# A mixture-of-experts layer whose leftover half groups are joined to pairs, as groups of three

## The chip, the cores and the metric

The kernel runs on one core of one Trainium2 chip. The time is the device time of one execution in microseconds, and the kernel before is given as the median of four runs. A core has five engines with queues of their own: TensorE (PE; its weight loads are listed as PEld), VectorE (DVE), ScalarE (ACT), GpSimd (POOL) and SyncE (SP), which here issues transfers only. POOL issues the transfers whose rows are chosen by a list.

## What is computed

A gated transformer layer on 8 x 512 tokens of width 256, everything in float32: cross-attention with 16 heads, then a router that sends each token to two of eight experts, each a two-layer network of inner width 1024.

```python
x = x + jnp.tanh(g_xattn[0]) * _L0_xattn_ref(_layernorm(x), ctx_1024, ctx_1024, mask, ...)
x = x + jnp.tanh(g_ffn[0]) * _L0_ffn_ref(_layernorm(x), router_w, router_b, expert_up, expert_down)

def _L0_ffn_ref(x, router_w, router_b, expert_up, expert_down):
    x_flat = x.reshape(-1, D)
    probs = jax.nn.softmax(x_flat @ router_w + router_b, axis=-1)
    top_w, top_idx = jax.lax.top_k(probs, TOP_K)
    comb = jnp.sum(top_w[..., None] * jax.nn.one_hot(top_idx, E, dtype=x.dtype), axis=1)
    output = jnp.zeros_like(x_flat)
    for e in range(E):
        h = jax.nn.gelu(x_flat @ expert_up[e].T, approximate=False)
        output = output + comb[:, e:e + 1] * (h @ expert_down[e].T)
    return output.reshape(B, S, D)
```

## The kernel before

**Attention, then experts, in one stream.** `attend_near` walks over the batches. While batch b's attention runs, the finished batch's rows are normalised and routed. Each routed token gets two entries in a table in memory, one for each expert it goes to; an entry says which row it is and with what weight it counts. The table has a region per expert, filled from its start (`filled` counts the rows of each expert so far). 64 indirect transfers on POOL (line 378) write it. It is first cleared by one transfer (`clear_table`, line 148), so that an empty slot points at no row.

**Groups.** The experts don't run over all tokens, but over groups of table rows of one expert. A half is 128 rows. A pair is two halves, 256 rows; a single is one half. Which groups exist is known only at run time, so `plan(k)` works it out with short VectorE operations for four kinds k: 5 pairs after three batches, 12 more pairs after six, 15 pairs after all eight, and then singles, of which the odd half of an expert makes one. Four singles always run (`OFTEN`), four more stand in a conditional block at the end (`compute_extra`, line 789), which is entered when more than four experts have an odd half. The plans give each group an expert (`whose_i`) and a place in the table (`line_i`).

**Jobs.** `JOBS` (lines 54 to 60) is the fixed order of the groups: 17 pairs, then 15 pairs with a single after the third, sixth, ninth and twelfth of them; 36 jobs in the main stream. The first four are mixed by hand into the attention of batches 4 to 7 (`amid`, line 1015). The others run after it (line 1087), the first of them interleaved with what is left of the last batches' routing (`queue`).

**One job.** `list_rows` (line 685) reads the group's table rows into `listed`; `load` (697) fetches the expert's two weight matrices, 1 MB each, both on SP's queue, into one of three buffers; `fetch` (713) gathers the token rows into `xg`, one POOL transfer per half; `turn` (719) transposes them on TensorE (line 724) and copies them to `xT` on DVE (726). `go_up` (729) does the first layer: 16 products, each two TensorE instructions (line 736), whose moving operand is as wide as the group has rows; ACT's Gelu (740) writes `hT`. `fetch_y` (742) gathers the rows of `out` that this group will add to. `go_down` (748) does the second layer for one half: 8 products of 128 x 128 weights against 256 columns, two TensorE instructions each (line 754), then DVE adds the weighted result to `y` (757) and POOL scatters `y` to `out` (760).

**Order.** `compute(s)` (line 771) sets the program order of a turn: gather rows of job s+2, gather `y` of job s-1, up of job s, transposes of job s+1, the downs of job s-1, list of job s+3, weights of job s+2. The framework places every instruction on its engine's queue by a schedule made from this order, and each queue is then worked in that order. All gathers of `y` read `out`, and all scatters write it, so a job's gathers wait for the scatters of the job before to land, and its scatters wait for its gathers. The scatters of the first and second halves go to views that are declared disjoint (`out_parts`, line 79).

**Banks.** The accumulators of a half's down (`o_ps`) come from `bank`, two buffers; those of up (`h_ps`) from five; the transposes' `x_ps` from one.

Of the kernel before, what the change touches and what calls it, by code (L numbers as in the profile page):

```python
# [10 lines left out]
F32 = mybir.dt.float32  # L11
# [8 lines left out]
P = 128  # L20
# [14 lines left out]

TOKENS = B * S
GROUP = 2 * P
PAIRS = 2 * TOKENS // GROUP
SINGLES = E

TABLE = TOKENS // GROUP


PARTS = (3, 6, B, B)
ENDS = [-(-(b * S * 2 - E * (GROUP - 1)) // GROUP) for b in PARTS[:2]] + [PAIRS]
SIZES = [ENDS[0], ENDS[1] - ENDS[0], ENDS[2] - ENDS[1], SINGLES]

OFTEN = SINGLES // 2

TABLES = E * TABLE + SIZES[2]  # L50

# [3 lines left out]
for _n in range(SIZES[2]):  # L55
    JOBS.append((2, _n))
    if _n % 3 == 2 and _n // 3 < OFTEN:
        JOBS.append((3, _n // 3))
MAIN = len(JOBS)
JOBS += [(3, n) for n in range(OFTEN, SINGLES)]  # L60
# [3 lines left out]
def flamingo_layer(ctx: ExitStack, tc: tile.TileContext, a: dict, out: bass.AP):  # L64
# [11 lines left out]
    table = tc.dram_tile([TABLES * GROUP, ENTRY], I32, name="table")  # L76

    table_parts = dram_disjoint_views(table, B * QT * 2)
    out_parts = dram_disjoint_views(out, 2)
# [68 lines left out]
    def clear_table(t):  # L148

        many = t.rearrange("p (n c) -> p n c", c=ENTRY)[:, : TABLES * GROUP // P // 11]  # L150
        nc.gpsimd.memset(many, 0)
        nc.gpsimd.memset(many[:, :, 0], TOKENS)
        nc.gpsimd.memset(many[:, :, 1], TOKENS - 1)
        n = many.shape[1]
        nc.sync.dma_start(
            out=table.rearrange("(p r n) c -> p r (n c)", p=P, n=n),
            in_=t[:, : n * ENTRY].unsqueeze(1).to_broadcast([P, TABLES * GROUP // P // n, n * ENTRY]),
        )
# [8 lines left out]
    full_i = mk.tile([P, 2 * TABLE], I32, tag="full_i", name="full_i")  # L167
    nc.gpsimd.iota(full_i, pattern=[[P, 2 * TABLE]], base=0, channel_multiplier=0)
    full = fixed([P, 2 * TABLE], "full")
# [13 lines left out]
    nc.vector.tensor_scalar(filled, iota, float(TOKENS), None, ALU.mult)  # L183
# [406 lines left out]
    def experts(pool, seen, half_bank, bank, row_bank):  # L590
# [6 lines left out]
        tables, loaded, fetched, turned, made, ys = {}, {}, {}, {}, {}, {}  # L597

        def halves(s):
            return 1 if JOBS[s][0] == 3 else 2  # L600

        def plan(k):
            n = SIZES[k]
            single = k == 3
            w = 1 if single else 2
            lines = 2 * TABLE // w

            def planned(shape, name, dtype=F32):
                return plans.tile(shape, dtype, tag=f"{name}{k}", name=f"{name}{k}")

            def scratch(shape, name):
                return plans.tile(shape, F32, tag=name, name=f"{name}{k}")

            def count():

                count = scratch([P, E], "count")
                nc.vector.scalar_tensor_tensor(count, iota, -float(TOKENS), filled, ALU.mult, ALU.add)  # L620
                if not single:
                    nc.vector.tensor_scalar(count, count, 1.0 - GROUP if k < 2 else -float(P), None, ALU.add)
                more = scratch([P, E, lines], f"more{lines}")
                nc.vector.tensor_tensor(
                    more, count.unsqueeze(2).to_broadcast([P, E, lines]),
                    full[:, ::w].unsqueeze(1).to_broadcast([P, E, lines]), ALU.is_gt,
                )
                groups = scratch([P, E + 1], "groups")
                nc.vector.memset(groups[:, E:], 0.0)
                nc.vector.tensor_reduce(groups[:, :E], more, AX.X, ALU.add)  # L630
                if k:
                    nc.vector.scalar_tensor_tensor(groups, tables["done"], -2.0 / w, groups, ALU.mult, ALU.add)
                ahead = scratch([P, E + 1, E], "ahead")
                nc.vector.tensor_tensor(
                    ahead, lower, groups[:, :E].unsqueeze(1).to_broadcast([P, E + 1, E]), ALU.mult
                )
                begin = scratch([P, E + 1], "begin")
                nc.vector.tensor_reduce(begin, ahead, AX.X, ALU.add)

                line = scratch([P, E + 1], "line")
                nc.vector.scalar_tensor_tensor(line, iota_e, float(lines), begin, ALU.mult, ALU.subtract)
                if k:
                    nc.vector.scalar_tensor_tensor(line, tables["done"], 2.0 / w, line, ALU.mult, ALU.add)
                past = scratch([P, n, E + 1], f"past{n}")
                nc.vector.tensor_tensor(
                    past, slot[:, :n].unsqueeze(2).to_broadcast([P, n, E + 1]),
                    begin.unsqueeze(1).to_broadcast([P, n, E + 1]), ALU.is_ge,
                )  # L650
                whose = scratch([P, n], f"whose{n}")
                nc.vector.tensor_reduce(whose, past, AX.X, ALU.add)
                whose_i = planned([P, n], "whose_i", I32)
                nc.vector.tensor_scalar(whose_i, whose, -1.0, float(E - 1), ALU.add, ALU.min)
                nc.vector.tensor_tensor(past, past, line.unsqueeze(1).to_broadcast([P, n, E + 1]), ALU.mult)
                far = scratch([P, n], f"far{n}")
                nc.vector.tensor_reduce(far, past, AX.X, ALU.max)
                line_i = planned([P, n], "line_i", I32)
                nc.vector.tensor_tensor(line_i, far, slot[:, :n], ALU.add)
                tables[k] = (whose_i, line_i, planned([P, n, w, FIELDS], "listed", I32))  # L660
                if single:
                    tables["extra"] = planned([P, 1], "extra", I32)
                    nc.vector.tensor_scalar(tables["extra"], begin[:, E:], float(OFTEN), None, ALU.is_gt)
                else:
                    done = planned([P, E + 1], "done")
                    nc.vector.tensor_scalar(done, begin, -1.0, float(n), ALU.mult, ALU.add)
                    nc.vector.tensor_scalar(done, done, 0.0, None, ALU.max)
                    nc.vector.tensor_tensor(done, done, groups, ALU.min)
                    if k:
                        nc.vector.tensor_tensor(done, done, tables["done"], ALU.add)  # L670
                    tables["done"] = done

            return count
# [11 lines left out]
        def list_rows(s):  # L685
            _, line_i, listed, n = planned_for(s)
            w = halves(s)
            lines = E * 2 * TABLE // w + SIZES[JOBS[s][0]]
            line = number(line_i, n, lines - 1)
            nc.sync.dma_start(  # L690
                out=listed[:, n],
                in_=table[: lines * w * P].rearrange("(r h p) c -> p r h c", h=w, p=P)[
                    :, bass.ds(line, 1), :, :FIELDS
                ].rearrange("p o h c -> p (o h) c"),
            )
# [16 lines left out]

        def fetch(s):
            xg = gather.tile([P, 2, D], F32, tag="xg", name=f"xg{s}")
            for h in range(halves(s)):
                rows_of(rows, s, h, xg[:, h, :])
            fetched[s] = xg

        def turn(s):
            xg, w = fetched.pop(s), halves(s)  # L720
            ps = row_bank(f"x_ps{s}").rearrange("p (c r) -> p c r", c=DC)
            for dc in range(DC):
                for h in range(w):
                    nc.tensor.transpose(ps[:, dc, h * P : (h + 1) * P], xg[:, h, dc * P : (dc + 1) * P], ident)  # L724
            xT = gather.tile([P, DC, GROUP], F32, tag="xT", name=f"xT{s}", bufs=2)
            nc.vector.tensor_copy(xT[:, :, : w * P], ps[:, :, : w * P])  # L726
            turned[s] = xT

        def go_up(s, f):
            up, xT, n = loaded[s][0], turned[s], halves(s) * P  # L730
            if f == 0:
                made[s] = hpool.tile([P, FC, GROUP], F32, tag="hT", name=f"hT{s}")
            ps = half_bank(f"h_ps{s}_{f}").rearrange("p (i r) -> p i r", i=2)
            for i in range(2):
                for dc in range(DC):
                    nc.tensor.matmul(  # L736
                        ps[:, i, :n], lhsT=up[:, dc, (f + i) * P : (f + i + 1) * P], rhs=xT[:, dc, :n],
                        start=(dc == 0), stop=(dc == DC - 1),
                    )
            nc.scalar.activation(made[s][:, f : f + 2, :n], ps[:, :, :n], AF.Gelu)  # L740

        def fetch_y(s):

            ys[s] = gather.tile([P, 2, D], F32, tag="y", name=f"y{s}", bufs=2)
# [20 lines left out]
        def ups(s):  # L765
            return [lambda f=f: go_up(s, f) for f in range(0, FC, 2)]
# [4 lines left out]
        def compute(s, end, first):  # L771
# [5 lines left out]
            if s + 1 < end:  # L777
                steps.append(lambda: turn(s + 1))
            if s > first:
                steps += downs(s - 1)  # L780
# [8 lines left out]
        def compute_extra():  # L789
            some = nc.values_load(  # L790
                tables["extra"][0:1, 0:1], min_val=0, max_val=1, skip_runtime_bounds_check_because="it is a comparison"
            )
            with tc.If(some == 1):
# [626 lines left out]
```

## Time and profile before

| what | value |
|---|---|
| median of 4 runs (848.88 to 855.85) | 851.57 us |
| the profiled execution | 850.44 us |
| its span, first to last instruction | 848.7 us |
| its mean granted TensorE clock | 0.954 |
| busy: PE, PEld, DVE, ACT, POOL | 766, 568, 328, 252, 314 us |
| up matmuls (L736), 1024 of 256 columns and 128 of 128 | 244.6 us |
| down matmuls (L754), 1088 of 256 columns | 244.1 us |
| gathers of rows, gathers of `y`, scatters | 68 each |
| loads of `up` and of `down`, 1 MB each | 36 each |

The span is the time from the first instruction to the last of one profiled execution; its whole time lies a little above it. Busy times of one engine are merged, so that overlapping matmuls count once. A group of instructions is listed by its line in the kernel, its engine, and the tile it writes and reads, such as `o_ps<-down,hT`; PE's own share is high over the whole span, but what ends last in a stage has to be read in that stage.

### The profile page before, as it was taken

To read this page: it belongs to the slowest core of one execution; us is meant where nothing else is said; L and a number is where in the kernel's file an instruction comes from. 1 tells how busy PE (TensorE), PEld (TensorE's weight loads), DVE (VectorE), ACT (ScalarE), POOL (GpSimd) and SP (SyncE) were. 2 spreads that over 40 slices of the span, in tenths; PEclk is the share of its full clock that TensorE was granted. 3 is DMA by queue.
4 is the path that set the end of the run, shared out by engine and by line. 5 is a ranking of instruction groups with operands and counts; after the bars stand their busy time and mean duration, and the time that the engine had idled before them with its cause. 6 is when DMAs were issued, how large, how long until landed. Compare 5 with 4: busy or idle time off the path is not lost. (4 is left out here: it accounts for less than half of the span.)

```text
span 848.7 us, 11331 instructions
## 1 busy us (share of the span) xinstructions
PE 765.9 (90%) x4090; PEld 567.9 (67%) x4090; DVE 327.6 (39%) x958; ACT 252.4 (30%) x485; POOL 313.6 (37%) x422
## 2 busy tenths in 40 slices
PE   3867989888899999899999799999999999999992
PEld 1333444434446575667787688888898988989882
DVE  7496887858865647525230111111111111011100
ACT  2434555444645435253311111111112111111210
POOL 2030115141645252444464544434342524434332
PEclk9897998989989998999999899999999999999996
DMA  4700000101293314061746656665667676757511
GB/s 143 259 7 1 32 32 29 50 29 51 88 312 99 105 53 125 4 205 50 258 138 209 200 202 214 201 207 203 194 205 236 196 240 210 227 174 258 199 50 36
DMA packets 87909, 121.58 MB, mean 143 GB/s; under 512 B 16797, under 2 KB 71712, under 8 KB 87840
## 3 DMA queue, kind: packets, MB, share of 16 engines
q1 hardware_dynamic: 75184, 93.44, 33.3%
q0 software_dynamic: 11840, 26.76, 10.1%
q8 instruction: 36, 0.59, 0.3%
q10 hardware_dynamic: 816, 0.53, 0.2%
q14 instruction: 33, 0.27, 0.1%
HBM read 101.05 MB, written 20.17 MB: 143 GB/s over the span
## 5 line engine op out<-in xcount | busy, mean ns | idle before, releaser
L754 PE MATMUL o_ps<-down,hT 128*128 128x256 f32 x1088 | 244.1, 382 | 8.7 <-DVE y L757 7.6
L736 PE MATMUL h_ps<-xT,up 128*128 128x256 f32 (+1 forms) x1152 | 244.6, 369 | 3.5 <-DMA up<-in_upT 1.8
L754 PEld LDWEIGHTS o_ps<-down,hT 128*128 128x128 f32 x1088 | 205.1, 191 | 40.8 <-DVE y L757 8.3
L736 PEld LDWEIGHTS h_ps<-xT,up 128*128 128x128 f32 x1152 | 208.7, 191 | 35.0 <-issue 6.0
L740 ACT ACTIVATE hT<-h_ps 128x512 f32<-128x512 f32 (+1 forms) x144 | 81.8, 573 | 363.6 <-PE h_ps L736 290.4
L757 DVE SCALAR_TENSOR_TENSOR y<-o_ps,listed,y 128x256 f32<-128x256 f32 x68 | 32.7, 483 | 274.9 <-DMA y<-out,listed 120.3
L708 POOL DMA_INDIRECT y<-out,listed x68 | 66.3, 975 | 165.1 <-DMA out<-y,listed 135.1
L760 POOL DMA_INDIRECT out<-y,listed x68 | 68.8, 1012 | 97.5 <-DVE y L757 70.2
L873 DVE TENSOR_REDUCE tops<-t_ps 128x4 f32<-128x512 f32 x128 | 79.4, 681 | 19.4 <-PE t_ps L868 16.0
L903 ACT ACTIVATE n_pT<-w_ps 128x512 f32<-128x512 f32 x128 | 67.5, 598 | 61.0 <-PE w_ps L898 37.3
L708 POOL DMA_INDIRECT xg<-rows,listed x68 | 64.8, 954 | 41.3 <-issue 18.5
L378 POOL DMA_INDIRECT table<-entries,place_i x64 | 62.7, 980 | 25.9 <-issue 16.5
L726 DVE COPY xT<-x_ps 128x512 f32<-128x512 f32 (+1 forms) x36 | 23.7, 658 | 106.4 <-PE x_ps L724 92.4
L898 PE MATMUL w_ps<-ql,km 32*128 32x512 f32 x256 | 54.9, 722 | 0.5 <-DVE tops L873 0.5
L868 PE MATMUL t_ps<-k,q 32*128 32x256 f32 x512 | 42.3, 404 | 3.0 <-ACT n_pT L903 1.6
L850 POOL TENSOR_TENSOR x<-x,bo 128x1024 f32<-128x1024 f32 x8 | 18.7, 2346 | 65.2 <-issue 34.5
L937 PE MATMUL proj_ps<-woT,oT 128*128 128x256 f32 x128 | 33.9, 403 | 9.8 <-DVE oT L930 9.8
L868 PEld LDWEIGHTS t_ps<-k,q 32*128 32x128 f32 x512 | 26.0, 185 | 24.7 <-issue 15.5
L916 PE MATMUL n_av<-n_pT,nv 128*32 128x512 f32 x256 | 39.1, 687 | 2.4 <-DVE xT L726 2.3
L922 DVE STREAM_TRANSPOSE raw<-n_av 128x512 f32<-128x512 f32 x32 | 22.8, 713 | 45.4 <-PE n_av L916 32.7
L937 PEld LDWEIGHTS proj_ps<-woT,oT 128*128 128x128 f32 x128 | 23.9, 197 | 21.8 <-DVE oT L930 11.4
L570 PE MATMUL q_ps<-n_xnT,wqT 128*128 128x512 f32 x64 | 34.6, 669 | 0.0
(187 smaller groups left out, 557.3 us busy)
## 6 DMA issues: line engine op xcount, KB each, us to landing
up<-in_upT SPq DMA_DIRECT2D x36, 1024.0 KB
down<-in_downT SPq DMA_DIRECT2D x36, 1024.0 KB
out<-x SPq DMA_DIRECT2D x8, 512.0 KB
rows<-xn_f SPq DMA_DIRECT2D x8, 512.0 KB
x<-in_x SPq DMA_DIRECT2D x7, 512.0 KB
table<-none SPq DMA_DIRECT2D x1, 2288.0 KB
xg<-rows,listed POOLq DMA_INDIRECT x68
y<-out,listed POOLq DMA_INDIRECT x68
```

The costliest lines, as they stand in the source:

```text
L378: nc.gpsimd.indirect_dma_start(out=table_parts[2 * t + i][:, :], out_offset=bass.IndirectOffsetOnAxis(ap=place_i[:, t, i : i + 1], axis=0) ...
L708: nc.gpsimd.indirect_dma_start(out=dst, out_offset=None, in_=src[: seen[JOBS[s][0]], :], in_offset=bass.IndirectOffsetOnAxis(ap=listed[:, ...
L736: nc.tensor.matmul(ps[:, i, :n], lhsT=up[:, dc, (f + i) * P : (f + i + 1) * P], rhs=xT[:, dc, :n], start=(dc == 0), stop=(dc == DC - 1),)
L740: nc.scalar.activation(made[s][:, f : f + 2, :n], ps[:, :, :n], AF.Gelu)
L754: nc.tensor.matmul(ps, lhsT=hT[:, f, h * P : (h + 1) * P], rhs=down[:, f, :], start=(f == 0), stop=(f == FC - 1))
L760: nc.gpsimd.indirect_dma_start(out=out_parts[h][:, :], out_offset=bass.IndirectOffsetOnAxis(ap=listed[:, n, h, 0:1], axis=0), in_=y[:, h, ...
L868: ins = nc.tensor.matmul(ps[j][:, u], lhsT=q[rows_j, c, t * P : (t + 1) * P], rhs=k[rows_j, c], start=True, stop=True)
L873: nc.vector.tensor_reduce(top[:, 2 * tp : 2 * tp + 2, :].rearrange("p t (i x) -> p t i x", i=2)[:, :, :, 32 * j], ps[j], AX.X, ALU.max,)
L898: ins = nc.tensor.matmul(ps[j], lhsT=km[rows_j, c, i, :], rhs=lowered[b, c][rows_j, i, :], start=True, stop=True)
L903: nc.scalar.activation(pT[:, j, :], ps[j], AF.Exp)
L916: ins = nc.tensor.matmul(av[32 * j : 32 * j + 32, :], lhsT=made_of(b)[3][:, 8 * c + 2 * j + r, :], rhs=pT[:, j, :], start=True, stop=True,)
L937: nc.tensor.matmul(ps[:, t - ts[0], :], lhsT=outs[b, c][:, t * P : (t + 1) * P], rhs=w["woT"][:, c, :], start=(c == 0), stop=(c == DC - 1),)
```

## The change

The fourth kind of group, the single, is gone. An expert with an odd number of halves has one group of three halves, a triple; all other groups are pairs. There are four places for triples (`TRIPLES`), and the kinds are now: 5 pairs, 12 pairs, 4 triples, 18 pairs. Of the last 18, 11 always run; three and then four more stand in two nested conditional blocks. `JOBS` is 17 pairs, then 11 pairs with a triple after the second, fifth, eighth and eleventh: 32 jobs in the main stream.

- The table's regions are 33 halves long (`SHARE`), so that a group may start at any half; `list_rows` reads as many halves as the group has.
- `plan_rest` takes the place of the last two plans; the steps common to all pairs are in `plan_pairs`.
- A triple's tiles (`xg`, `y`, `xT`, `hT`) come from a pool of their own, `wide`, with one buffer each, in the room of the attention's working pools, which are now closed when `queue` is empty.
- Its up runs over 384 columns, one product of eight at a time to a bank instead of two; its transposes go in two steps, each with its own copy, the second after the first half's down; it has three downs.

```diff
-SIZES = [ENDS[0], ENDS[1] - ENDS[0], ENDS[2] - ENDS[1], SINGLES]
-OFTEN = SINGLES // 2
+SIZES = [ENDS[0], ENDS[1] - ENDS[0], TRIPLES, 2 * TOKENS // GROUP + E - 1 - TRIPLES - ENDS[1]]
+OFTEN = SIZES[3] - 7
+MORE = OFTEN + 3
+LINES = E * SHARE + 2 * SIZES[3]
...
-for _n in range(SIZES[2]):
-    JOBS.append((2, _n))
-    if _n % 3 == 2 and _n // 3 < OFTEN:
-        JOBS.append((3, _n // 3))
+for _n in range(OFTEN):
+    JOBS.append((3, _n))
+    if _n % 3 == 1 and _n // 3 < TRIPLES:
+        JOBS.append((2, _n // 3))
...
-    out_parts = dram_disjoint_views(out, 2)
+    out_parts = dram_disjoint_views(out, 3)
...
         def halves(s):
-            return 1 if JOBS[s][0] == 3 else 2
+            return 3 if JOBS[s][0] == 2 else 2
...
+        def plan_rest():
+            count = count_rows(2)
...
+            pairs, whole = each("pairs"), each("whole")
+            nc.vector.tensor_reduce(pairs, more[:, 0], AX.X, ALU.add)
+            nc.vector.tensor_reduce(whole, more[:, 1], AX.X, ALU.add)
+            left, odd = each("left"), each("odd")
+            nc.vector.tensor_tensor(left, pairs, tables["done"][:, :E], ALU.subtract)
+            nc.vector.tensor_tensor(odd, pairs, whole, ALU.subtract)
+            three = each("three")
+            nc.vector.scalar_tensor_tensor(three, left, 2.0, odd, ALU.is_ge, ALU.mult)
...
+            nc.vector.tensor_tensor(groups[:, :E], left, saved, ALU.subtract)
+            begin = plan_pairs(3, groups)
...
+        def turn_wide(s, dc):
+            n = halves(s) * P
+            if dc == 0:
+                turned[s] = wide[0].tile([P, DC, n], F32, tag="xT3", name=f"xT{s}")
+            ps = row_bank(f"x_ps{s}_{dc}")[:, :n]
+            for h in range(n // P):
+                nc.tensor.transpose(ps[:, h * P : (h + 1) * P], fetched[s][:, h, dc * P : (dc + 1) * P], ident)
+            nc.vector.tensor_copy(turned[s][:, dc], ps)
+
+        def go_up(s, f, m):
             up, xT, n = loaded[s][0], turned[s], halves(s) * P
             if f == 0:
-                made[s] = hpool.tile([P, FC, GROUP], F32, tag="hT", name=f"hT{s}")
-            ps = half_bank(f"h_ps{s}_{f}").rearrange("p (i r) -> p i r", i=2)
-            for i in range(2):
+                where = hpool if n == GROUP else wide[0]
+                made[s] = where.tile([P, FC, n], F32, tag=f"hT{n}", name=f"hT{s}")
+            ps = half_bank(f"h_ps{s}_{f}")[:, : m * n].rearrange("p (i r) -> p i r", i=m)
+            for i in range(m):
                 for dc in range(DC):
                     nc.tensor.matmul(
-                        ps[:, i, :n], lhsT=up[:, dc, (f + i) * P : (f + i + 1) * P], rhs=xT[:, dc, :n],
+                        ps[:, i, :], lhsT=up[:, dc, (f + i) * P : (f + i + 1) * P], rhs=xT[:, dc, :],
                         start=(dc == 0), stop=(dc == DC - 1),
                     )
...
         def ups(s):
-            return [lambda f=f: go_up(s, f) for f in range(0, FC, 2)]
+            m = 512 // (halves(s) * P)
+            return [lambda f=f: go_up(s, f, m) for f in range(0, FC, m)]
+
+        def turns(s):
+            if halves(s) == 2:
+                return [lambda: turn(s)]
+            return [lambda dc=dc: turn_wide(s, dc) for dc in range(DC)]
...
-            if s + 1 < end:
-                steps.append(lambda: turn(s + 1))
-            if s > first:
-                steps += downs(s - 1)
+            turned_next = turns(s + 1) if s + 1 < end else []
+            steps += turned_next[:1]
+            last = downs(s - 1) if s > first else []
+            steps += last[:1] + turned_next[1:] + last[1:]
...
                 if queue:
                     queue.popleft()()
+                    if not queue:
+                        heads.close()
+                        open_wide()
```

## The prediction, made before the changed kernel was run

> **What bounds the kernel now.** First the page's busy slices: each of the 40 is 21.2 us.
>
> ```profile
> PE   3867989888899999899999799999999999999992
> PEclk9897998989989998999999899999999999999996
> ```
>
> From slice 24 on (about 470 us) TensorE stands at 9 and its granted clock at 9: the expert stage is bound by TensorE. Next the chain of waits, in order of time (start, us, what): it says whether that stage's end really hangs on PE.
>
> ```profile
> 473.07 9.01 PE o_ps L754 x32
> 482.08 6.91 PE h_ps L736 x32
> 488.99 0.44 PE x_ps L724 x4
> 489.43 6.91 PE o_ps L754 x32
> ...
> 717.72 0.22 PE x_ps L724 x2
> 717.94 6.91 PE o_ps L754 x32
> 724.85 3.57 PE h_ps L736 x32
> ```
>
> It does: a pair costs 6.91 us up (L736), 6.91 down (L754) and 0.44 of transposes (L724), 14.26 in all; a single 3.57, half of 6.91 and 0.22. Then the busy table by stage (stretch; its length, then PE, PEld, DVE, ACT, POOL busy; clock; DMA share; GB/s), to find where PE still waits.
>
> ```profile
> 692.00:720.00 28.00, 27.81 (x134) 24.27 (x133) 4.04 (x8) 5.37 (x9) 9.82 (x10) 1.00 0.64 212
> 720.00:750.00 30.00, 28.64 (x153) 25.48 (x152) 3.13 (x6) 3.92 (x8) 12.74 (x13) 1.00 0.61 200
> ```
>
> From 474 us to the last matmul these are the only stretches short of full: 0.19 and 1.36 us. The timeline says what PE waited for, and shows the loop that competes with it:
>
> ```profile
> 603.28 0.98 POOL L708 DMA_INDIRECT y<-out,listed  x1 [5.37 <-issue]
> 608.35 1.02 POOL L760 DMA_INDIRECT out<-y,listed  x1 [0.30 <-issue]
> 611.20 1.00 POOL L760 DMA_INDIRECT out<-y,listed  x1 [1.83 <-DVE y L757]
> 619.60 0.98 POOL L708 DMA_INDIRECT y<-out,listed  x1 [7.40 <-DMA out<-y,listed]
> ...
> 744.47 3.72 PE L754 MATMUL o_ps<-down,hT 128*128 128x256 f32 x16 [1.36 <-DVE y L757]
> ```
>
> A job's y gathers (L708) wait until the scatters (L760) of the job before have landed, and its scatters wait for its gathers. Among pairs, last scatter to next gather took 6.3 to 8.9 us, gather to add (L757) about 3.0, and y0, y1, xg0, xg1, then the first scatter start 1.27 apart on POOL (603.28 to 608.35). That loop closes in about 13.4 us (626.00 to 638.88 is 12.88; 664.23 to 677.87 is 13.64), just under the pair's 14.26, so the first half's add runs only 0.2 to 2.2 us after its matmuls end. A single breaks this: at 638.88 the loop took 16.2 us and then 9.2 (second scatter of one pair 638.88, single's 655.03, next pair's last 664.23), 25.4 against 21.5 of PE work. From 692 to 812 us the first half's add was on average 7.0 us late (up to 11.8), and twice PE found both of its o_ps banks taken.
>
> **What the change does to this, part by part.** Routing the reference's inputs gives the experts 6, 9, 6, 10, 8, 9, 11 and 9 halves: 68, four odd, which agrees with 68 gathers of each kind and with 32 pairs and 4 singles. After: 28 pairs and 4 triples, 68 halves again. Rounded up they are 36 pairs; 17 are listed early, 8 go into triples, and 11 are left, exactly OFTEN, so no extra job runs.
>
> *Up.* Four singles and four pairs (4 x 3.57 + 4 x 6.91 = 41.92 us) become four triples. Triples by the pair's cost per column: 6.91 x 1.5 = 10.37 each, 41.46; by the line through 128 and 256 columns: 10.25, 41.0. Gain 0.46 to 0.92; I take 0.5, since 256 columns is nearer to 384.
>
> The Trainium skill (TensorE: Matmul & The Clock Gate, Back-to-back issue gap) says that the spacing of matmuls is set by weight load and stream together, about 81 ns at 128 columns and 131 at 512. By that line the three widths would cost 81, 98 and 114 ns, and four triples for four singles and four pairs, 128 instructions of each, would save an estimated 8.3 us. The trace does not agree: 112 ns at 128 columns against 216 at 256, nearly proportional.
>
> *Down and transposes.* 48 matmuls instead of 32 and 16; 12 transposes instead of 8 and 4: nothing. ACT makes eight Gelus of 384 columns per triple where the rows give 0.38 for 256 and 0.60 for 512; one falls under each four matmuls of 1.3 us. DVE's two copies of 384 columns lie between 0.42 and 0.69 each, under the downs; if that cover went, they would cost PE 1.1 per triple.
>
> *The waits that singles cause.* 0.19 + 1.36 = 1.55 us, 1.6 rounded, bounds 0 (they return elsewhere) and 1.6. I take 1.6: beside a triple PE works 6.91 + 10.37 + 0.5 = 17.8 us per turn, and the loop with a third gather (1.27) and third scatter (1.3) is about 16.
>
> *The new waits.* A triple's third down needs the bank of its own first half, free 3.46 us after the first half's matmuls end. The add there ends at lateness + 0.48, so a lateness of 0.2 to 2.2 costs nothing. The second copy of xT3 stands behind that add in the program order of DVE: 2.2 + 0.48 + 0.55 = 3.2 under 3.46 plus the transposes. On POOL a triple's three row gathers hold the scatters behind them 1.27 back, in a turn that still has 7.92 (603.28 to 611.20) for its last scatter: 7.6. Taken 0; bounds 0 and 0.6 for each of three triples.
>
> *Transfers.* Eight transfers of 1 MB fewer on SP's queue (`up` and `down` of four jobs); PE waits 1.8 us for `up` in the whole trace, so nothing on the path. Lists: one DMA per job as before.
>
> *The planning.* The last plan grows from 36 to 43 short DVE operations, 7 x 0.2 = 1.4 us, between 430 and 440 us; the jobs that read it begin some 150 us later, and the adds and copies of the stage have 7 us of down matmuls over them. The two early plans gain three operations (3 x 0.17 = 0.5) where DVE stands at 7 to 8 tenths. The cleared table grows from 286 to 300 blocks, 112 KB, 0.4 us at the 260 to 320 GB/s of that stage. I take 0.3 lost, bounds 0 and 0.9.
>
> *The end.* The last job is now a triple.
>
> ```profile
> 826.30 0.48 DVE L757 SCALAR_TENSOR_TENSOR y<-o_ps,listed,y 128x256 f32<-128x256 f32 x1 [2.97 <-PE o_ps L754]
> 830.31 0.98 POOL L708 DMA_INDIRECT y<-out,listed  x1 [2.25 <-DMA out<-y,listed]
> 833.41 0.48 DVE L757 SCALAR_TENSOR_TENSOR y<-o_ps,listed,y 128x256 f32<-128x256 f32 x1 [6.63 <-DMA y<-out,listed]
> 836.46 1.00 POOL L760 DMA_INDIRECT out<-y,listed  x1 [0.30 <-issue]
> ```
>
> Call T the end of the next-to-last job's downs (826.10). T comes 3.46 earlier, since one half more lies behind it. The add of the last job's first half starts at T + 7.3 as now; its third down can begin when that add is done, T + 7.8, takes 3.46, and its scatter follows about 1.0 later, T + 12.3 instead of T + 10.36. From the last scatter to the end 12.24 stay. Gain 3.46 - 1.95 = 1.5, bounds 0.5 and 2.
>
> Sum: -0.5 - 1.6 + 0 + 0.3 - 1.5 = -3.3 us on a span of 848.7: 845.4. The profiled execution took 850.44 in all, 1.7 more than its span and 0.13% under the median of 851.57. The same ratio on the median gives **848.3 us**. With all bounds taken at once: -4.5 to +1.7, 847.1 to 853.3.
>
> **The rivals.**
>
> *The triple ties PE to the gather loop (slower).* Now the same job's add frees the bank for its third half, where a pair has a whole turn of slack. If lateness stays at the 7.0 us of the singles' stage, each of three triples stalls 7.0 + 0.48 - 3.46 = 4.0, 12 us: 860. It beats the gain once lateness at triples passes 3.46 - 0.48 + 3.3/3 = 4.1. For it: ten of the eleven first halves from 692 us on were above 2.6. Against it: those followed singles, and the pairs before 603 us worked lateness off by about 0.9 per turn. The Trainium skill (TensorE: Matmul & The Clock Gate, Architectural detail) has VectorE's queue as strict FIFO, which speaks against this change: the copy of xT3 would wait with the add. No run here shows a copy in that place yet.
>
> *Weight loads count (much faster).* TensorE loads 1024 weights for up instead of 1152, 128 fewer; at their full 191 ns that is 24 us: 827. Against it stands 3.57 beside 6.91.
>
> *The order shifts at the last routing.* At 473 us the chain shows PE idle for 6.3 us, at 459 for 2.1, while POOL alternates between table scatters and job DMAs. The order of each engine is set by the scheduler; a longer plan can move an add there. One place in POOL's order is worth 1.3 us, three of them 4: 844 or 852, either way.
>
> *It doesn't do what it says.* With more than 11 pairs left, three extra jobs of 14.26 would run: 891. The counts exclude it.
>
> **How the numbers follow.** What a measurement of this kernel can tell from no change is 0.5%, 4.3 us. Forecast 0.66: its lower bound just passes -4.3 and the four runs shown scatter by 7 us, so 0.21 faster, 0.43 within, 0.02 slower. Loop rival 0.20: 0.14 slower, 0.06 within, when only one or two triples stall. Order rival 0.09: 0.05 faster, 0.01 within, 0.03 slower. Weight loads 0.04, faster. Extra jobs 0.01, slower. Faster 0.30, within 0.50, slower 0.20. The likeliest one's own range is 847.1 to 853.3; the one that holds 8 in 10 reaches down to 844 (order rival) and up to 857, where the loop rival costs two thirds of its price.
>
> **What would show it right or wrong.** Right: h_ps of 384 columns at 10.3 to 10.4 us per triple; no PE gap over 0.3 us from 474 us to the last `up`; the first half's add at most 2.2 us after its matmuls everywhere; at the end a gap of about 0.9 us before the third half's downs. Wrong: PE gaps of several us ahead of a triple's third half or of the `up` of a triple; a copy of xT3 behind a waiting add; a stage before 474 us that ends more than 2 us earlier or later.

## The result, and the profile after

The changed kernel takes 847.65 us (median of 38 runs) against 851.19 (59 runs): ratio 0.9955, 95% interval 0.994 to 0.997, 3.8 us faster where 3.3 were forecast. The ratio leaves out slow executions; the two medians, which don't, differ by 3.5. Two more groups of runs gave 0.998 (0.9942 to 1.0019) and 0.9962 (0.9934 to 0.9991). The profiled execution has a span of 844.9 us.

From the page of the changed kernel: the busy slices of PE with the granted clock, and the two groups of matmuls.

```profile
PE   3877989888899999999998799999999999999992
PEclk9898998888899998999999899999999999999997
...
L848 PE MATMUL o_ps<-down,hT 128*128 128x256 f32 x1088 | 245.0, 383 | 8.6 <-DVE y L851 7.5
L830 PE MATMUL h_ps<-xT,up 128*128 128x256 f32 (+1 forms) x1024 | 242.6, 393 | 3.3 <-DVE oT L1041 1.7
```

The expert stage is as full as it was. Down has the same 1088 matmuls; up has 1024 instead of 1152, but its busy time falls only from 244.6 to 242.6. From the chain of waits, in order of time (start, us, what), one triple:

```profile
601.34 0.33 PE x_ps L818 x3
601.67 3.46 PE o_ps L848 x16
605.13 0.33 PE x_ps L818 x3
605.45 3.46 PE o_ps L848 x16
608.91 10.32 PE h_ps L830 x32
619.23 0.44 PE x_ps L807 x4
619.67 6.91 PE o_ps L848 x32
...
633.92 10.36 PE o_ps L848 x48
```

Its transposes lie around the first down of the job before (601 to 605), its up takes 10.32 us, its three downs 10.36, and PE never waits. At each triple but the last, the first half's add runs as soon as its matmuls end, as here:

```profile
637.41 0.48 DVE L851 SCALAR_TENSOR_TENSOR y<-o_ps,listed,y 128x256 f32<-128x256 f32 x1 [2.77 <-PE o_ps L848]
```

The table by stage agrees (stretch; its length, then PE, PEld, DVE, ACT, POOL busy; clock; DMA share; GB/s): where the kernel before had 0.19 and 1.36 us of idle PE, every stretch from 600 to 800 us is full. One of them:

```profile
720.00:760.00 40.00, 40.00 (x176) 32.18 (x175) 4.13 (x8) 7.53 (x15) 14.11 (x15) 1.00 0.57 183
```

The end is another matter. The timeline of the changed kernel from the next-to-last job's second add (818.47) on:

```profile
818.47 0.48 DVE L851 SCALAR_TENSOR_TENSOR y<-o_ps,listed,y 128x256 f32<-128x256 f32 x1 [2.97 <-PE o_ps L848]
...
822.48 0.98 POOL L785 DMA_INDIRECT y<-out,listed  x1 [2.25 <-DMA out<-y,listed]
823.77 0.97 POOL L785 DMA_INDIRECT y<-out,listed  x1 [0.30 <-issue]
825.05 0.95 POOL L785 DMA_INDIRECT y<-out,listed  x1 [0.30 <-issue]
...
826.03 3.72 PE L848 MATMUL o_ps<-down,hT 128*128 128x256 f32 x16 [0.70 <-DVE y L851]
...
828.57 1.02 POOL L854 DMA_INDIRECT out<-y,listed  x1 [2.56 <-DMA y<-out,listed]
829.79 0.48 DVE L851 SCALAR_TENSOR_TENSOR y<-o_ps,listed,y 128x256 f32<-128x256 f32 x1 [2.75 <-PE o_ps L848]
829.89 1.01 POOL L854 DMA_INDIRECT out<-y,listed  x1 [0.30 <-issue]
831.20 0.99 POOL L854 DMA_INDIRECT out<-y,listed  x1 [0.30 <-issue]
```

The third down does wait for the bank (826.03), but the last scatter does not wait for it: POOL issues three gathers 1.28 apart, holds the first scatter until the third gather has landed, and issues three scatters 1.31 apart. Its queue ends later than the third add at 829.79.

Then POOL waits for the last scatter to land. Each line below gives POOL's waits at the very end (shortest, median and longest, in ns); the longest is the wait for that landing. The lines are from the kernel before, the changed kernel, and the kernel before with the longer gather loop of the experiments:

```profile
L793 POOLq EVENT_SEMAPHORE  x4: 17/43/2270, 836.7 to 839.2; - x4
L908 POOLq EVENT_SEMAPHORE  x5: 17/43/3471, 831.5 to 835.3; - x5
L796 POOLq EVENT_SEMAPHORE  x4: 17/43/4090, 850.6 to 854.9; - x4
```

From the start of the last scatter (836.46, 831.20 and 850.33) to the end of that wait are 2.6, 4.0 and 4.4 us. What follows the landing takes 9.6 to 9.8 us in all 14 profiles.

Three profiles of either kernel, cut at two points: "start" is where PE's 6.3 us gap after the last routing ends, T the end of the next-to-last job's downs.

| kernel, profile | start | start to T | T to end | start to end |
|---|---|---|---|---|
| before, first | 473.07 | 353.03 | 22.63 | 375.65 |
| before_2 | 466.62 | 351.77 | 22.70 | 374.47 |
| before_3 | 468.73 | 352.87 | 22.68 | 375.55 |
| changed, first | 470.49 | 347.77 | 26.68 | 374.45 |
| after_2 | 471.71 | 347.88 | 26.84 | 374.72 |
| after_3 | 470.11 | 347.45 | 27.30 | 374.76 |

Start to end agrees within 1.2 us from profile to profile of one kernel, the start itself scatters by 6.5. In the stage that the change is about, the mean falls from 375.2 to 374.6 us: 0.6, not 3.8.

### The profile page after: what moved, and what is told of

It reads as the page before. It is cut to its first block, busy times and chain, and to the rows that moved or that the text cites. A ratio compares the mean times of both kernels' runs of the same rounds, so it can differ in the third digit from the quotient of the medians.

```text
span 844.9 us, 10980 instructions
## 1 busy us (share of the span) xinstructions
PE 766.7 (91%) x3962; PEld 553.8 (66%) x3962; DVE 328.3 (39%) x968; ACT 252.4 (30%) x485; POOL 314.7 (37%) x422
## 4 chain that ended last, share of the span: by engine, by line
PE 67%; DVE 14%; issue 5%; SPq 3%; DMA 3%; ACT 2%; POOL 1%; another core or an unknown queue 0%; POOLq 0%; DVEq 0%; ACTq 0%
PE h_ps L830 24%; PE o_ps L848 24%; DVE tops L984 4%; PE w_ps L1009 4%; PE n_av L1027 3%; PE proj_ps L1048 3%; SPq L769 3%; PE t_ps L979 2%; PE q_ps L572 2%; PE top_ps L997 1%; DVE n_o L1036 1%; PE x_ps L807 1%; DVE ql L998 1%; DMA out<-y,listed 1%; DMA y<-out,listed 1%
## 5 line engine op out<-in xcount | busy, mean ns | idle before, releaser
L830 PE MATMUL h_ps<-xT,up 128*128 128x256 f32 (+1 forms) x1024 | 242.6, 393 | 3.3 <-DVE oT L1041 1.7
L830 PEld LDWEIGHTS h_ps<-xT,up 128*128 128x128 f32 x1024 | 193.2, 190 | 46.4 <-issue 5.0
L809 DVE COPY xT<-x_ps 128x512 f32<-128x512 f32 x28 | 19.3, 689 | 135.6 <-PE x_ps L807 120.1
L1009 PE MATMUL w_ps<-ql,km 32*128 32x512 f32 x256 | 58.1, 745 | 0.4 <-DVE tops L984 0.4
L572 PE MATMUL q_ps<-n_xnT,wqT 128*128 128x512 f32 x64 | 32.3, 631 | 0.2 <-ACT k L559 0.2
```

The lines of the kernel that those rows point to most:

```text
L830: nc.tensor.matmul(ps[:, i, :], lhsT=up[:, dc, (f + i) * P : (f + i + 1) * P], rhs=xT[:, dc, :], start=(dc == 0), stop=(dc == DC - 1),)
L1009: ins = nc.tensor.matmul(ps[j], lhsT=km[rows_j, c, i, :], rhs=lowered[b, c][rows_j, i, :], start=True, stop=True)
```

## The experiments

The theory: TensorE bounds the expert stage, and the change is worth what it takes from PE's columns and waits there, less what the longer last job costs at the end. The rivals: a triple ties PE to the loop of gathers and scatters; singles cost nothing beyond their matmuls; the gain comes from the planning, the table or the closed pools rather than from the groups.

**Both kernels again** (before_2, after_2, later before_3, after_3; no edit).

> The kernel before, unchanged, profiled once more. Theory: the 2.6 us by which the changed kernel reached the expert stage earlier (470.5 against 473.1 us) is scatter between executions, since the order on every engine up to there is the same but for the plans; this profile then reaches that point anywhere between 469 and 476 us, the ratio is 1.000 within its interval, and PE again waits 1 to 4 us for an o_ps bank between 680 and 770 us, in jobs that follow a single. Rival: the earlier start belongs to the change; then this profile stands at 473 again within 0.5 us.

Measured: 0.9982 (0.9938 to 1.0025). Start at 466.62, ahead of the 469 to 476 expected and 6.5 us ahead of the first profile of the same kernel, so the start scatters by more than the 2.6 us in question. PE's waits for banks came to 0.19 us, less and later than the 1 to 4 expected:

```profile
786.76 1.56 PE L754 MATMUL o_ps<-down,hT 128*128 128x256 f32 x6 [0.19 <-DVE y L757]
```

> The changed kernel, unchanged, profiled once more. Theory: 0.9955 of the time before; no PE gap over 0.3 us between the first 10 us of the expert stage and the last up; first halves added at most 1 us late at every triple; from the end of the next-to-last job's downs to the end of the span 26 us, as in the first profile. Rival (the triple ties PE to the gather loop): lateness over 3 us at some triple and a gap ahead of its third half.

Measured: 0.998 (0.9942 to 1.0019); no gap between start and the last up, the first half's add 0.2 us late at each triple of the stream, 26.84 us from T to the end.

> The kernel before, unchanged, third profile, beside the changed kernel on one chip. Theory: ratio 1.000 within its interval; 374 to 376 us from the start of the expert stage (the end of its 6.3 us gap) to the end of the span; 0 to 2 us of PE waiting for o_ps banks after singles. Rival: the time before that stage is longer here than in the changed kernel by 2 us or more.

Measured: 1.001 (0.9978 to 1.0043); 375.55 us from start to end, and one wait of 1.28 us:

```profile
689.97 1.35 PE L754 MATMUL o_ps<-down,hT 128*128 128x256 f32 x5 [1.28 <-DVE y L757]
```

> The changed kernel, unchanged, third profile. Theory: 0.994 to 0.998 of the time before; 374.4 to 374.8 us from the start of the expert stage to the end of the span, of which 26.7 after the next-to-last job's downs; the start of that stage within 3 us of that of the kernel before on the same chip, either way.

Measured: 0.9962 (0.9934 to 0.9991); 374.76 us, of which 27.30 after T. The starts of the two, 468.73 and 470.11, don't explain a faster kernel.

**The last job a pair** (after_lastpair, after_lastpair_2).

```diff
-    if _n % 3 == 1 and _n // 3 < TRIPLES:
+    if _n % 3 == 0 and _n // 3 < TRIPLES:
```

> The changed kernel with each triple one pair earlier, so that the last job is a pair. Theory: the end after the next-to-last job's downs shrinks from 26.4 to 22.4 us as in the kernel before, and one half more lies ahead of it (3.46): 0.5 us faster than the changed kernel, 0.995 of the time before. Rival (the 4 us at the end have to do with the nested conditional blocks and not with the third half): the end stays above 24 us and the kernel becomes 1 to 2 us slower than the changed one.

Measured: 0.9973 (0.9933 to 1.0014), T to end 22.72 us, start to end 373.69. So the 4 us belong to the third half of the last job, not to the nested conditional blocks, which are still there.

> The changed kernel with a pair as its last job, once more, beside the changed kernel on the same chip. Theory: 1.0 us faster than the changed kernel by the profiles (373.7 against 374.6 us from the start of the expert stage to the end), 0.993 to 0.997 of the time before. Rival: no faster than the changed kernel.

Measured: 0.9959 (0.993 to 0.9989); 372.94 us from start to end. By the profiles it beats both kernels, by 1.3 us on the changed one (373.3 against 374.6); by the times it can't be told from it (845.52 and 846.26 us beside each other).

**Singles at the end of the stream** (before_singles_end): the four singles of the kernel before run one after another.

```diff
-    if _n % 3 == 2 and _n // 3 < OFTEN:
-        JOBS.append((3, _n // 3))
+JOBS += [(3, _n) for _n in range(OFTEN)]
```

> The kernel before with its four singles moved behind all 15 pairs, nothing else: the same matmuls. Theory (a single's turn has 7.25 us of PE work, but its loop of gather, add, scatter and landing takes some 12): the lateness of the adds grows by about 5 us per single and PE stalls there 5 to 12 us in all, while the waits between 690 and 750 us vanish (-1.6) and the end after a single is about 2 us shorter net: 1.003 to 1.01. Rival (singles cost no more than their matmuls): no new gaps, and the shorter last job makes it 1 to 2 us faster, 0.998.

Measured: 1.0076 (1.0041 to 1.011): singles do cost more than their matmuls. The time is in the range of the theory, but its mechanism isn't what happened: PE waited only 0.65 us in the stream, not 5 to 12, and the rest showed at the end, 29.36 us from T on. The chain there:

```profile
829.71 5.04 DMA y<-out,listed
...
834.93 0.50 DVE y L756
...
835.69 1.00 POOL out L759
...
838.27 2.78 DMA y<-out,listed
```

Gather, landing, add, scatter, landing, and again: a single's whole loop in a row, with no matmul in it.

**Triples closer together** (after_dense): one pair between two triples, three pairs at the end.

```diff
-    if _n % 3 == 1 and _n // 3 < TRIPLES:
-        JOBS.append((2, _n // 3))
+    if _n % 2 == 1 and _n // 2 < TRIPLES:
+        JOBS.append((2, _n // 2))
```

> The changed kernel with its triples after the second, fourth, sixth and eighth of the last 11 pairs instead of the second, fifth, eighth and eleventh: one pair between two triples, and three pairs at the end. Theory (TensorE bounds the stage, and beside a triple it works 17.8 us per turn against a gather loop of 16): no new gap between first and last up, lateness under 2 us, the stage as long as with the last job a pair (373.7 us from its start to the end of the span), 0.995 to 0.998 of the time before. Rival (a triple ties PE to the gather loop): lateness builds over the dense triples, gaps of 1 us or more ahead of third halves, 2 to 6 us slower than the changed kernel.

Measured: 0.9949 (0.9926 to 0.9971), on another chip, where the kernel before takes 833.09 us. No gap, lateness at most 1.0 us, start to end 373.92. The rival fails where it should show most.

**A longer gather loop in both kernels** (before_long_loop, after_long_loop).

```diff
             for h in range(halves(s)):
                 rows_of(out, s, h, ys[s][:, h, :])
+            if s >= 17:
+                mine = ys[s][:, : halves(s), :]
+                nc.vector.tensor_scalar(mine, mine, 1.0, None, ALU.mult)
```

> The kernel before, with the gather loop lengthened in the last 19 jobs: VectorE multiplies each gathered y by one ahead of the adds, which has to wait for all its gathers. The outputs stay the same. Theory (singles cost waits because their loop does not shrink with their matmuls): a pair's loop grows by about 1.1 us to 14.5, a single's two turns from 25.4 to 27.6 against 21.5 of PE work; some 6 us of lateness per single, four of them less the 10 us that the banks cover: PE waits 10 to 18 us for o_ps banks from 650 us on, 1.012 to 1.02 of the time before. Rival (the waits that a single causes are worth nothing): under 1.003.

Measured: 1.0345 (1.0304 to 1.0387), more than expected, and not for the reason given. The timeline of before_long_loop:

```profile
629.19 0.98 POOL L708 DMA_INDIRECT y<-out,listed  x1 [7.63 <-DMA out<-y,listed]
...
636.21 0.29 DVE L749 TENSOR_SCALAR y<-y 128x256 f32<-128x256 f32 x1 [16.86 <-DMA xg<-rows,listed]
636.41 0.68 DVE L726 COPY xT<-x_ps 128x512 f32<-128x512 f32 x1
...
637.15 3.35 PE L736 MATMUL h_ps<-xT,up 128*128 128x256 f32 x7 [9.03 <-DVE xT L726]
```

The single's multiplication waits for its gather (issued at 629.19, it lands at 636.11; the row names the transfer of rows issued behind it), the next job's copy of xT waits behind it on DVE, and PE waits for the copy: 9.0 us here, 23.6 at the four singles together. It was not the o_ps banks. So it shows what a late loop costs at a single, with a wait that neither kernel has of itself.

> The changed kernel with the same multiplication by one in the last 15 jobs. Theory: pairs lose 0.3 us per turn, a triple's turns win back 0.7 or more; PE waits at most 2 us, 0 to 2 us slower than the changed kernel, and 8 to 16 us faster than the kernel before with the same lengthening. Rival (the triple ties PE to the gather loop, so that a longer loop hits it harder than the kernel before): gaps ahead of third halves, slower than the kernel before with the lengthening.

Measured: 1.0155 (1.0103 to 1.0207), 842.67 us: 18.8 faster than the kernel before with the same edit, but some 13 slower than the changed kernel, where 0 to 2 were expected. (The changed kernel has no run on that chip; its 829.3 there is an estimate, 0.9955 of 833.09.) TensorE's weight loads for the triples' second transposes wait 7.4 us in all for the one bank of x_ps, whose first copy stands behind the multiplication; the end grows by 4 to 30.8 us; and two of the three third halves in the stream wait, as here:

```profile
692.34 1.99 PE L851 MATMUL o_ps<-down,hT 128*128 128x256 f32 x8 [0.92 <-DVE y L854]
```

The first half's add was 4.0 us late there, and the rival's price says 4.0 + 0.48 - 3.46 = 1.0, where 0.92 was measured. So the rival's mechanism exists at its price; in the changed kernel, where the first half's add is 0.2 us late at each triple of the stream, its condition is never met.

**The last job a single** (before_last_single).

```diff
-    if _n % 3 == 2 and _n // 3 < OFTEN:
-        JOBS.append((3, _n // 3))
+    if _n % 3 == 2 and _n // 3 >= 1:
+        JOBS.append((3, _n // 3 - 1))
```

> The kernel before with its four singles one place later each, after the sixth, ninth, twelfth and fifteenth of the 15 pairs, so that the last job is a single. Theory (each half of the last job costs the end a gather of 1.28, a scatter of 1.31 and 1.4 of landing, all on POOL and its transfers): from the end of the next-to-last job's downs to the end of the span 18.7 us where a pair has 22.7 and a triple 26.7. Rival (what the triple's end lost is its third down waiting for the bank, 3.5 us that a single does not have either way): 21.4 us, the pair's less one gather.

Measured: 1.0022 (0.9997 to 1.0047), and 22.49 us from T to the end: both expectations miss. The timeline of POOL there:

```profile
811.70 0.98 POOL L708 DMA_INDIRECT y<-out,listed  x1 [2.51 <-DMA out<-y,listed]
816.72 1.00 POOL L760 DMA_INDIRECT out<-y,listed  x1 [4.03 <-DVE y L757]
```

The only gather (811.70) lands in 4.1 us by the chain of waits, where the last one of the kernel before takes 2.7, and 13.0 us follow the last scatter instead of 12.3. What the missing gather and scatter save, these two take back. So the end is not a fixed price per half. Why this gather lands later is open; being alone doesn't make it so, since the last single's gather in before_singles_end landed in 2.78 us.

**The planning without the triples** (after_split): planning, table and closed pools as changed, each triple run as a pair and later a single.

```diff
-    JOBS.append((3, _n))
-    if _n % 3 == 1 and _n // 3 < TRIPLES:
-        JOBS.append((2, _n // 3))
+    _pairs.append((3, _n))
+    if _n % 3 == 1 and _n // 3 < TRIPLES:
+        _pairs.append((2, _n // 3))
+for _n, _job in enumerate(_pairs):
+    JOBS.append(_job)
+    if _n % 3 == 2 and _n // 3 < TRIPLES:
+        JOBS.append((4, _n // 3))
...
-            return 3 if JOBS[s][0] == 2 else 2
+            return 1 if JOBS[s][0] == 4 else 2
...
+            nc.vector.tensor_scalar(line_1, sums[:, 1], float(E * SHARE + 2), None, ALU.add)
+            tables[4] = (whose_i, line_1, planned(4, [P, n, 1, FIELDS], "listed", I32))
```

> The changed kernel with its planning, table and closed pools, but each triple run as a pair and, some jobs later, a single of the same expert: 15 pairs and 4 singles in the order of the kernel before, with 36 loads of weights. Theory (what is gained lies in the groups): 0.998 to 1.002 of the time before, adds up to 8 us late after singles, 375 us or more from the start of the expert stage to the end, of which 22.7 after the next-to-last job's downs. Rival (the gain comes from the planning, the table or the pools closed early): as fast as the changed kernel, 0.995.

Measured: 0.9973 (0.9946 to 1.0), between the two theories and told from neither. Adds run up to 9.1 us late after singles, as in the kernel before; 374.12 us from start to end (375 or more was expected), 22.89 of them after T; PE waited for no bank in this execution. So the groups of three are not shown to be the whole of the gain.

## Why the prediction was right, point by point

The forecast of 848.3 us met 847.65, and no change beyond 0.5% was the right call. Its sum was not as good as its total.

- **Up: right.** A triple takes 10.32 us, between the 10.25 and 10.37 of the two lines: 4 x (3.57 + 6.91 - 10.32) = 0.64 gained, 0.5 forecast. The wide matmuls cost 322 ns beside 112 and 216 at 128 and 256 columns, so the 128 weight loads saved are worth next to nothing and that rival falls. The spacing of the Trainium skill (TensorE: Matmul & The Clock Gate, Back-to-back issue gap), far from proportional, would have given the estimated 8.3 us; the trace does not agree with it for these matmuls. (The prediction's 12, 8 and 4 transposes are 6, 4 and 2 in the trace; the sums are equal either way.)
- **The waits after singles: right mechanism, smaller size.** The adds ran up to 11.8, 10.6 and 11.7 us late after singles in the three profiles of the kernel before, and PE waited 1.55, 0.19 and 1.28 us: 1.0 on average, not 1.6. In the changed kernel they are gone.
- **The new waits: right.** None, in three profiles and with the triples closer together. The bank was priced as it turned out when a longer loop was forced (0.92 for 1.0). There the triples' second transposes also waited for the first copy, a wait that the prediction doesn't name.
- **The end: the step that failed.** "From the last scatter to the end 12.24 stay. Gain 3.46 - 1.95 = 1.5": it was a loss. T to end grew by 4.3 (26.9 on average against 22.7), 0.8 more than the 3.46 that T came earlier. Two parts were mis-sized. The last scatter came at T + 13.0 instead of T + 12.3. The prediction hung it on the third down; but the first scatter waits for the third gather, as the prediction itself says of the loop, and one gather and one scatter more, 10.36 + 1.28 + 1.31, make 12.95. And 13.7 to 14.3 us follow it instead of 12.2 to 12.3, because the last scatter lands 4.0 to 4.5 us after its start instead of 2.5 to 2.6. With a pair as the last job both parts go back, which is shown. Why the scatter lands later is open: three scatters instead of two can't be the whole reason, since the second of two took 4.4 us in before_long_loop.
- **The planning: not settled.** 0.3 lost was forecast for it. Up to the start, PE, ACT, POOL and SP work the same instructions in the same order in both kernels, and DVE has ten more, all in the plans.
- **The order at the last routing: no shift.** PE's gap there is in all six profiles of the table (idle for 6.01 to 6.34 us before, 6.09 to 6.26 changed). One sign that the prediction gave for being wrong did come up, a start more than 2 us earlier (470.49 against 473.07), but it can't tell the kernels apart: the kernel before itself scatters from 466.6 to 473.1.

The terms as measured, -0.64 - 1.0 + 0.8, make -0.8 us from the start of the expert stage to the end, and the profiles say -0.6. The times say -3.8 (-5.1 to -2.6). So about 3 us of the measured gain, or what the intervals leave of it, lie outside the steps that were forecast, and the number was met partly by luck. It is not in the expert stage. It isn't seen ahead of it either: leaving out the quicker chip, four profiles with the old planning reach the start at 466.6 to 473.1 us (469.5 on average), six with the new at 470.1 to 472.2 (471.1). Nor do the profiled executions show the gain as a whole: those three of the kernel before took 846.5 us on average, those of the changed kernel 847.2. The run with the changed planning and no triples leaves room for the planning, the table or the closed pools, but its interval reaches 1.0 and its start, 471.61, is not early. This stays open; a few profiles with 6 us of scatter ahead of the stage can't settle it.

## What to carry to other kernels

When a unit of work is too small to cover a fixed loop of transfers, joining it to a larger one removes lateness, but on a path bound by TensorE only the waits that PE really has count, and here they were about 1 us. What comes last counts: the gathers and scatters of the last job lie bare at the end, and a third half there cost about what the removal of singles had won. A single half there won nothing over a pair, though (22.5 against 22.7 us), so measure the end instead of pricing it by the half. When a total comes out right, compare its terms with the trace all the same.

## What the runs showed of the hardware

- **The time varies with the granted clock by more than this change is worth.** 45 runs of the kernel before on one chip had a mean granted clock of 0.944 to 0.967; a line through them gives 6.5 us for each 0.01, and 2.3 us of scatter remain about it. The idle end counts in that mean (0.50 from 836 us on in the first profile of the kernel before), so kernels with different ends can't be compared at equal clock. Another chip ran the same kernel in 833.09 instead of 850.92 us; the four variants profiled there reached the expert stage at 452 to 456 us.
- **VectorE keeps its order even when the first in line waits.** With the added multiplication, a copy of xT whose transposes were done at 624.7 us ran only at 636.4, right behind it, and PE waited for 9.0 us of that. The Trainium skill (TensorE: Matmul & The Clock Gate, Architectural detail: the array is 16x 32x32, not 1x 128x128) calls that queue strict FIFO; the trace agrees, with 23.6 us of PE waiting for four such copies.
- **The end of a kernel hangs on how the last scatter lands.** It landed 4.0 to 4.5 us after its start as the third of three, 2.5 to 2.7 as the second of two in seven profiles but 4.4 in one (before_long_loop), and 3.1 and 3.4 where it followed over 6 us behind the one before. 9.6 to 9.8 us from there to the end of the span were the same in all.
